# The scan's first token: VectorE's addition in PSUM replaced by a state from GpSimd that ScalarE copies in

## The chip, the cores and the metric

The kernel runs on one core of a Trainium2 chip. A core has five engines with a queue each: TensorE (PE in the profile, PEld for its weight loads), VectorE (DVE), ScalarE (ACT), GpSimd (POOL) and SyncE (SP), whose queue issues the DMAs here. Each queue is worked off in order; the engines meet only at semaphores. Matmul results land in PSUM; everything else lives in SBUF. The metric is the device time of one execution in microseconds, the median of several runs. A time of this kernel is told from no change at about 0.2%.

## The reference: what is computed

A state-space layer, then a gated feed-forward layer, each with a residual and a layer norm. For two sequences of 1024 tokens, model width 512 and state width N = 128:

```
xn    = rmsnorm(x) * norm_w ;  xn = xn * sigmoid((xn @ sel.T + b) * gate)
delta, B, C = split(xn @ x_proj.T)              # 128, 128, 128 wide
dt    = softplus(delta @ dt_proj.T + dt_b)      # 512 wide
A     = -exp(A_log)                             # 512 x 128
h_t   = exp(dt_t * A) * h_(t-1) + (dt_t * xn_t) B_t^T     # 512 x 128 per token
y_t   = h_t C_t
x     = layernorm(x + (y + x * D_param) @ out_proj.T)
x     = layernorm(x + (silu(x @ wg.T) * (x @ wu.T)) @ wd.T)   # hidden 2048
```

The state `h` is zero at the start of each sequence. All is fp32.

## The kernel before

**Tiling of the scan.** State column n lies on the partition, so a scan instruction has 128 partitions. Time is cut into 64 steps of S = 32 tokens (32 steps per sequence). A step `st` has two halves `i`, a half covers 256 of the 512 channels, and a half is worked in 8 iterations `r` = 0..7 of 32 channels each. The main loop thus has 1024 iterations `k`; here "half-step" means 8 of them. In one scan instruction (L660) 32 channels x 32 tokens lie one behind the other, 1024 elements. So that a channel does not run on into the next, the decay factor of each first token in `a_sb` is zero; the scan therefore starts every channel from the first token's entry in `bu`, and what the previous step left must already be in that entry.

**One iteration.** TensorE makes two things, each in two matmuls of 512 columns that sit in 32-row groups: `bu` (L644) from the diagonal tiles `du` and the row tile `ub`, and the exponent's argument `a` (L377) for the *next* iteration from `ddt` and `a_t`. Their order in the queue is bu, a, bu, a; this is called a block below. ScalarE turns `a` into decay factors in two `Exp` instructions (L384) into one of three buffers of `a_sb`, tokens 1 to 31 only. VectorE adds the carried state into the first token of `bu` in PSUM (L657, 128x32), then scans (L660) into `h`. Four PSUM banks hold two buffers of `bu` (L644 of iteration k+2 must wait for the scan of k), and two banks hold `a` (a matmul must wait for the Exp of the same half of the iteration before).

**The carried state.** `load(st)` (L302 on) fetches for the next step the rows `ub` (eight DMAs, L310 and L313) and `cd`, the first token's `dt` spread over 128 partitions (L320), and copies C into `cz` (L315). `carry_a` makes `cd = exp(a_n * cd)`: a product on GpSimd (L326) and an Exp on ScalarE (L327), at iteration 5 of the first half. `carry_h` (L335) multiplies half of `cd` by the last token of `h` of the step before, on GpSimd, at iteration 1 of the half ahead of the one that needs it. L657 adds a slice of the product. The first step of each sequence (`st % NSB == 0`) carries nothing and has no L657.

**Other work.** GpSimd builds `ddt` and `du` (L348, L358): one 128x512 product per iteration, two of each kind in four iterations. `y_round` (L396) multiplies finished states by `cz` at iterations 1, 4 and 7 of the next half. A hand-written list of generators, `work`, fills TensorE's remaining time: `PARTS = (4, 0, 3, 3, 0, 3, 3, 0)` says how many parts (matmuls, roughly) are taken after each iteration's block, with a credit that carries over up to 6. A generator yields `"H"` between parts, `"E"` where other engines must act first, `"P"` where it wants the one spare PSUM bank. Through it run `pre` (the projections of the next 256 tokens, 8 chunks; the B projection is L240 with the copy L246), `post` (L429 to L459) and `ffn` (L469 on: `gu` L500, `d` L518, `silu`). The order on every queue is the order in which this program issues; nothing reorders it.

Of the kernel before, what the change touches and what calls it, by code (L numbers as in the profile page):

```python
# [9 lines left out]
FP = mybir.dt.float32  # L10
AF = mybir.ActivationFunctionType
ALU = mybir.AluOpType
# [3 lines left out]
P = 128  # L16
S = 32
TC = 256
# [16 lines left out]
def kernel(  # L35
# [17 lines left out]
    nc = tc.nc  # L53
# [3 lines left out]
    B, L, D = out.shape  # L57
    NTT = B * L // P
    N = a_log.shape[2]
    R = dtw_t.shape[0]  # L60
    NF = wgu_s.shape[0]
    NM = D // P
    NH = NF // 2
    NJ = TC // P
    HD = D // 2
    NSB = L // S
    NS = B * NSB
    SPC = TC // S
# [10 lines left out]
    u_d = dram.tile([B * L, D], FP, name="u_d")  # L79
# [29 lines left out]
    xp_w = main.tile([P, NM, R + 2 * N], FP, name="xp_w")  # L109
# [6 lines left out]
    pre_pool = tc.alloc_tile_pool(name="pre", bufs=1)  # L116
    step_pool = tc.alloc_tile_pool(name="step", bufs=2)
# [34 lines left out]
    made = {}  # L152
# [3 lines left out]
    def misc(name):  # L156
        return bank_pool[0].tile([P, 512], FP, tag="m", name=name)
# [5 lines left out]
    def pre(c):  # L163
# [7 lines left out]
        low = pre_pool.tile([P, TC], FP, tag="low", name=f"low_{c}")  # L171
        dt = pre_pool.tile([P, NM, TC], FP, tag="dt", name=f"dt_{c}", bufs=2)
        u = pre_pool.tile([P, NM, TC], FP, tag="u", name=f"u_{c}")
        c_sb = pre_pool.tile([P, TC], FP, tag="c_sb", name=f"c_sb_{c}", bufs=2)
        made[c] = dt, c_sb
        xn = xT

        def matmuls(ps, w, m, rhs):
# [13 lines left out]
        ps = misc(f"ss_{c}")  # L192
# [19 lines left out]
        for m in range(NM):  # L212
            ps = misc(f"sel_{c}_{m}")
# [17 lines left out]
        for g, dst in ((0, low), (2, c_sb)):  # L231
            ps = misc(f"xp_{c}_{g}")
# [4 lines left out]
        ps = misc(f"b_{c}")  # L237
        for j in range(NJ):
            for k in range(NM):
                nc.tensor.matmul(  # L240
                    ps[:, ts(j, N)], xn[:, k, ts(j, P)], xp_w[:, k, R : R + N],
                    start=(k == 0), stop=(k == NM - 1),
                )
            yield "H" if j + 1 < NJ else "E"
        bt = pre_pool.tile([P, NJ, N], FP, tag="bt", name=f"bt_{c}")
        nc.scalar.copy(bt, ps[:, 0:TC].rearrange("p (j n) -> p j n", j=NJ))  # L246
        nc.sync.dma_start(b_d[ts(c, TC), :].rearrange("(j p) n -> p j n", p=P), bt)
        yield "P"

        for a in range(0, NM, 2):  # L250
            ps = misc(f"z_{c}_{a}")
# [14 lines left out]
        for j in range(NJ):  # L266
            yield "P"
            ps = misc(f"uT_{c}_{j}")
# [5 lines left out]
            t = pre_pool.tile([P, D], FP, tag="row", name=f"uT_{c}_{j}")  # L274
# [3 lines left out]
        ps = misc(f"t0_{c}")  # L278
        for m in range(NM):
# [3 lines left out]
                start=True, stop=True,  # L283
            )
        yield "E"
        t = pre_pool.tile([P, D], FP, tag="row", name=f"t0_{c}")
# [12 lines left out]
    def toks(st):  # L299
        return ts(st % SPC, S)  # L300

    prepared, carried, dus, ddts, hs, ys = {}, {}, {}, {}, {}, {}  # L302

    def load(st):


        ub = step_pool.tile([P, 2, P], FP, tag="ub", name=f"ub_{st}")
        rows = u_d[ts(st, S), :].rearrange("t (m g c) -> g t m c", g=4, c=32)
        for g in range(4):
            nc.sync.dma_start(  # L310
                ub[ts(g, S), 0, :].rearrange("t (m c) -> t m c", c=32), rows[g]
            )
            nc.sync.dma_start(ub[ts(g, S), 1, :], b_d[ts(st, S), :])  # L313
        prepared[st] = ub
        nc.gpsimd.tensor_copy(  # L315
            cz[st % 3][:, 28:284].rearrange("p (b w) -> p b w", w=32)[:, :, 0:4],
            made[st // SPC][1][:, toks(st)].rearrange("p (b t) -> p b t", t=4),
        )
        cd = step_pool.tile([P, D], FP, tag="cd", name=f"cd_{st}")
        nc.sync.dma_start(cd, dt0_d[st : st + 1, :].to_broadcast([P, D]))  # L320
        carried[st] = cd

    def carry_a(st):

        cd = carried[st]
        nc.gpsimd.tensor_tensor(cd, a_n, cd, ALU.mult)  # L326
        nc.scalar.activation(cd, cd, AF.Exp)  # L327

    def carry_h(st, i):

        if st % NSB == 0:
            return
        cd = carried[st].rearrange("p (b i e) -> p b i e", i=2, e=16)[:, :, i, :]
        last = hs[2 * (st - 1) + i][:, :, S - 1].rearrange("p (b e) -> p b e", e=16)
        nc.gpsimd.tensor_tensor(cd, cd, last, ALU.mult)  # L335

    def diag(j, part):

        h, a = j // 2, 2 * (j % 2)
        if h >= 2 * NS:  # L340
            return
        st, i = divmod(h, 2)
        name, m = divmod(part, 2)
        shape = [P, 2, 16, S]
        if name == 0:
            if m == 0:
                ddts[j] = half_pool.tile(shape, FP, tag="ddt", name=f"ddt_{j}")
            nc.gpsimd.tensor_tensor(  # L348
                ddts[j][:, m, :, :],
                made[st // SPC][0][:, a + m, toks(st)].unsqueeze(1).to_broadcast([P, 16, S]),  # L350
                hot[:, ts(i, 16)].unsqueeze(2).to_broadcast([P, 16, S]),
                ALU.mult,
            )
        else:
            if m == 0:
                dus[j] = half_pool.tile(shape, FP, tag="du", name=f"du_{j}")
            uv = prepared[st][:, 0, :].rearrange("p (m i e) -> p m i e", i=2, e=16)[:, :, i, :]
            nc.gpsimd.tensor_tensor(  # L358
                dus[j][:, m, :, :],
                uv[:, a + m, :].unsqueeze(2).to_broadcast([P, 16, S]),  # L360
                hot.unsqueeze(1).to_broadcast([P, 16, S]),
                ALU.mult,
            )
# [3 lines left out]
    def place(k):  # L367
        h, r = divmod(k, 8)
        m, pair = divmod(r, 2)
        return h, m, pair  # L370

    def decay_mm(k, b):

        h, m, pair = place(k)
        g = 2 * pair + b
        ps = ps_a.tile([P, 16, S], FP, tag="a", name=f"a_{k}_{b}")
        nc.tensor.matmul(  # L377
            ps, a_t[ts(g, 32), m, :], ddts[k // 4][ts(g, 32), m % 2, :, :],
            start=True, stop=True,
        )  # L380
        return ps

    def decay_exp(k, b, ps):
        nc.scalar.activation(  # L384
            a_sb[:, k % 3, ts(b, 16), 1:], ps[:, :, 1:], AF.Exp
        )
# [235 lines left out]
    for k in range(NG):  # L622
        h, m, pair = place(k)
        st, i = divmod(h, 2)
        r = k % 8
        work.others()
        if r == 0:
            hs[h] = half_pool.tile([P, 256, S], FP, tag="h", name=f"h_{h}")

            if i == 1 and st:  # L630
                y_out(st - 1)
            if i == 0:
                if st % SPC == 0 and st // SPC + 1 < NC:
                    pres[st // SPC + 1] = work.add(pre(st // SPC + 1), front=True)
                if st + 1 < NS:
                    if (st + 1) % SPC == 0:
                        work.finish(pres[(st + 1) // SPC])
                    load(st + 1)

        bu = ps_bu.tile([P, 32, S], FP, tag="bu", name=f"bu_{k}")  # L640
        nxt = []
        for b in range(2):
            g = 2 * pair + b
            nc.tensor.matmul(  # L644
                bu[:, ts(b, 16), :], prepared[st][ts(g, 32), 1, :],
                dus[k // 4][ts(g, 32), m % 2, :, :],
                start=True, stop=True,
            )
            if k + 1 < NG:
                nxt.append(decay_mm(k + 1, b))  # L650
        if nxt:
            decay_exp(k + 1, 0, nxt[0])
        if st % NSB:
            left = carried[st].rearrange("p (b i e) -> p b i e", i=2, e=16)
            first = bu[:, :, 0].rearrange("p (b e) -> p b e", e=16)
            at = 4 * m + 2 * pair
            nc.vector.tensor_tensor(first, first, left[:, at : at + 2, i, :], ALU.add)  # L657
        if nxt:
            decay_exp(k + 1, 1, nxt[1])
        nc.vector.tensor_tensor_scan(  # L660
            hs[h][:, ts(r, 32), :].rearrange("p q t -> p (q t)"),
            a_sb[:, k % 3, :, :].rearrange("p q t -> p (q t)"),
            bu.rearrange("p q t -> p (q t)"),
            0.0, ALU.mult, ALU.add,
        )
        if h:
            for b in ROUNDS[r]:
                y_round(h - 1, b)
        credit = min(credit + PARTS[r], 6)
        while PARTS[r] and credit > 0 and work.tensor():  # L670
            credit -= 1

        j, r4 = divmod(k, 4)
        if r4 == 3:
            diag(j + 2, 0)
        else:
            diag(j + 1, r4 + 1)
        if r == 1:
            if i == 0 and st:
                carry_h(st, 1)  # L680
            if i == 1 and st + 1 < NS:
                carry_h(st + 1, 0)
        if r == 5 and i == 0 and st + 1 < NS:
            carry_a(st + 1)
# [81 lines left out]
```

## Time and profile before

Median of three runs 2960.17 us (2959.35 to 2963.21).

| | |
|---|---|
| profiled execution, its own time | 2962.62 us |
| its span | 2960.8 us |
| TensorE busy | 2757.0 us (93%) |
| VectorE busy | 2526.3 us (85%), of it the scan 2340.8 (1024 x 2287 ns) and the addition L657 183.7 (992 x 185 ns) |
| GpSimd busy | 1842.1 us (62%) |
| ScalarE busy | 1545.2 us (52%), of it the Exps of `a_sb` 1089.4 |
| first scan starts, last scan ends | 97.7, 2847 us |

How to read it: the span has a head of 98 us (the first chunk's projections, no scan), a loop of 2750 us, and a tail of 113 us in which TensorE finishes the feed-forward layer alone. In the loop, up to about 475 us, there is no feed-forward work yet; after that TensorE has side work in nearly every half-step. Busy shares are averages over these stages.

### The profile page before, as it was taken

What the parts mean: (1) busy time and instruction counts of PE and PEld (TensorE: products, weight loads), DVE (VectorE), ACT (ScalarE), POOL (GpSimd) and SP (SyncE); (2) the same over time, 40 slices, a digit from 0 to 9 for tenths busy, and PEclk for the clock granted to TensorE, in tenths of its full rate; (3) what the DMA queues carried; (4) which work ended last, traced back from release to release, by engine and by line L of the source; (5) the groups of instructions that cost most, each with busy time, mean ns of one, the idle gap of its engine ahead of it and who ended that gap; (6) DMA issues with size and microseconds to landing.
All of it is one profiled execution on the core that took longest, in us unless ns stands there. A gap on an engine that the chain in (4) does not pass through costs nothing.

```text
span 2960.8 us, 53130 instructions
## 1 busy us (share of the span) xinstructions
PE 2757.0 (93%) x20608; PEld 1388.5 (47%) x20608; DVE 2526.3 (85%) x2176; ACT 1545.2 (52%) x3043; POOL 1842.1 (62%) x1970
## 2 busy tenths in 40 slices
PE   3787779999999998999999999999999999999988
PEld 2332324545444444444444454444444545454457
DVE  0599999999888998999999999999998999999940
ACT  2454445645465464664555555555555545454533
POOL 2465556766657575675666766576666757665744
PEclk7699999999999999999999999999999999999999
DMA  1000001212112111112111111111211212122123
GB/s 60 26 19 19 11 26 37 62 62 61 35 49 65 46 61 41 50 55 69 46 47 60 54 58 60 49 51 38 76 47 39 74 54 62 49 61 63 55 79 121
DMA packets 110458, 155.11 MB, mean 52 GB/s; under 512 B 46784, under 2 KB 69824, under 8 KB 110208
## 3 DMA queue, kind: packets, MB, share of 16 engines
q1 hardware_dynamic: 110208, 151.72, 16.7%
q8 instruction: 164, 2.69, 0.4%
q14 instruction: 86, 0.70, 0.1%
HBM read 142.09 MB, written 9.57 MB: 51 GB/s over the span
## 4 chain that ended last, share of the span: by engine, by line
PE 70%; DVE 20%; issue 4%; POOL 2%; ACT 2%; DMA 1%; SPq 0%; DVEq 0%; POOLq 0%; ACTq 0%
PE bu L644 25%; DVE h L660 17%; PE gu L500 16%; PE y L396 12%; PE d L518 6%; PE a L377 5%; PE sel L180 1%; DVE bu L657 1%; PE op L443 1%; PE xp L180 1%; ACT a_sb L384 1%; PE b L240 1%; PE ss L194 0%; DMA w<-in_wd_s_dram 0%; POOL dt L296 0%
## 5 line engine op out<-in xcount | busy, mean ns | idle before, releaser
L660 DVE TENSOR_TENSOR_SCAN h<-a_sb,bu 128x1024 f32<-128x1024 f32 x1024 | 2340.8, 2287 | 217.0 <-PE bu L644 100.0
L384 ACT ACTIVATE a_sb<-a 128x496 f32<-128x496 f32 x2048 | 1089.4, 585 | 1129.7 <-PE a L377 976.1
L644 PE MATMUL bu<-du,ub 32*128 32x512 f32 x4096 | 1213.5, 648 | 77.2 <-DVE h L660 43.7
L377 PE MATMUL a<-ddt,a_t 32*128 32x512 f32 x4096 | 1262.6, 649 | 13.4 <-POOL ddt L348 12.8
L348 POOL TENSOR_TENSOR ddt<-dt,hot 128x512 f32<-128x512 f32 x512 | 534.6, 1050 | 337.4 <-PE a L377 337.3
L358 POOL TENSOR_TENSOR du<-ub,hot 128x512 f32<-128x512 f32 x512 | 535.9, 1052 | 52.0 <-PE a L377 49.5
L644 PEld LDWEIGHTS bu<-du,ub 32*128 32x128 f32 x4096 | 343.9, 185 | 477.7 <-issue 283.7
L396 PE MATMUL y<-h,cz 128*32 128x256 f32 x8192 | 531.1, 389 | 1.6 <-DVE h L660 1.6
L500 PE MATMUL gu<-x1T,w 128*128 128x256 f32 x2048 | 518.7, 395 | 5.7 <-ACT x1T L488 2.8
L500 PEld LDWEIGHTS gu<-x1T,w 128*128 128x128 f32 x2048 | 368.7, 190 | 253.2 <-issue 178.3
L396 PEld LDWEIGHTS y<-h,cz 128*32 128x32 f32 x8192 | 229.6, 110 | 415.8 <-issue 305.6
L377 PEld LDWEIGHTS a<-ddt,a_t 32*128 32x128 f32 x4096 | 384.5, 185 | 42.1 <-ACT a_sb L384 21.8
L534 POOL TENSOR_SCALAR gu<-gu 128x256 f32<-128x256 f32 x128 | 108.7, 849 | 314.0 <-ACT gu L506 313.9
L518 PE MATMUL d<-w,hid 128*128 128x256 f32 x1024 | 261.8, 397 | 20.2 <-DMA w<-in_wd_s_dram 10.0
L657 DVE TENSOR_TENSOR bu<-bu,cd 128x32 f32<-128x32 f32 x992 | 183.7, 185 | 111.9 <-PE a L377 106.9
L518 PEld LDWEIGHTS d<-w,hid 128*128 128x128 f32 x1024 | 185.6, 192 | 145.5 <-issue 92.3
L410 POOL TENSOR_TENSOR yc<-yc,pick 128x512 f32<-128x512 f32 x64 | 66.6, 1041 | 155.9 <-ACT yc L409 155.9
L335 POOL TENSOR_TENSOR cd<-cd,h 128x256 f32<-128x256 f32 x124 | 106.6, 859 | 64.3 <-DVE h L660 64.3
L540 POOL TENSOR_TENSOR hid<-gu,e 128x256 f32<-128x256 f32 x128 | 93.6, 731 | 26.5 <-ACT e L539 23.9
L524 DVE TENSOR_TENSOR x<-x,d 128x256 f32<-128x256 f32 x64 | 25.5, 399 | 94.3 <-PE d L518 94.3
L535 POOL TENSOR_TENSOR gu<-gu 128x256 f32<-128x256 f32 x128 | 94.5, 738 | 10.7
L506 ACT COPY gu<-gu 128x512 f32<-128x512 f32 x128 | 75.3, 588 | 38.9 <-PE gu L500 38.9
(86 smaller groups left out, 1292.0 us busy)
## 6 DMA issues: line engine op xcount, KB each, us to landing
w<-in_wgu_s_dram SPq DMA_DIRECT2D x128, 512.0 KB, 4.1
w<-in_wd_s_dram SPq DMA_DIRECT2D x64, 512.0 KB, 4.1
cd<-dt_d SPq DMA_DIRECT2D x64, 256.0 KB, 4.3
xT<-in_x_t_dram SPq DMA_DIRECT2D x8, 512.0 KB, 5.2
u_d<-uT SPq DMA_DIRECT2D x16, 256.0 KB, 2.2
ub<-u_d SPq DMA_DIRECT2D x256, 16.0 KB, 2.0
ub<-b_d SPq DMA_DIRECT2D x256, 16.0 KB, 1.9
zT<-in_x_q_dram SPq DMA_DIRECT2D x16, 256.0 KB, 5.9
```

What stands on the lines that cost most here:

```text
L335: nc.gpsimd.tensor_tensor(cd, cd, last, ALU.mult)
L348: nc.gpsimd.tensor_tensor(ddts[j][:, m, :, :], made[st // SPC][0][:, a + m, toks(st)].unsqueeze(1).to_broadcast([P, 16, S]), hot[:, ts(i, ...
L358: nc.gpsimd.tensor_tensor(dus[j][:, m, :, :], uv[:, a + m, :].unsqueeze(2).to_broadcast([P, 16, S]), hot.unsqueeze(1).to_broadcast([P, 16, ...
L377: nc.tensor.matmul(ps, a_t[ts(g, 32), m, :], ddts[k // 4][ts(g, 32), m % 2, :, :], start=True, stop=True,)
L384: nc.scalar.activation(a_sb[:, k % 3, ts(b, 16), 1:], ps[:, :, 1:], AF.Exp)
L396: nc.tensor.matmul(ys[st][ts(m, 32), ts(i, 256)], cz[st % 3][:, at : at + 32], hs[h][:, ts(m, 64), ts(b, 4)], start=(i == 0 and b == 0), s ...
L500: nc.tensor.matmul(ps[:, ts(a, TC)], w[:, a, k, :], x1T[:, k, :], start=(k == 0), stop=(k == NM - 1),)
L518: nc.tensor.matmul(ps[:, 0:HD], hid[:, f, ts(j, P)], w[:, f % 4, :], start=(f == 0), stop=(f == NH - 1),)
L534: nc.gpsimd.tensor_scalar_max(g, g, -80.0)
L644: nc.tensor.matmul(bu[:, ts(b, 16), :], prepared[st][ts(g, 32), 1, :], dus[k // 4][ts(g, 32), m % 2, :, :], start=True, stop=True,)
L657: nc.vector.tensor_tensor(first, first, left[:, at : at + 2, i, :], ALU.add)
L660: nc.vector.tensor_tensor_scan(hs[h][:, ts(r, 32), :].rearrange("p q t -> p (q t)"), a_sb[:, k % 3, :, :].rearrange("p q t -> p (q t)"), b ...
```

## The change

The first token's complete state is now made ahead. TensorE multiplies, in a third group at the end of the B projection, each step's first token alone: four matmuls with 8 moving columns per chunk, into 8 spare columns of the same bank; the group before it now yields `"H"` and takes one more part. ScalarE copies the 8 columns to `b0` (128x8). `load` fetches `cu`, the first token's row of `u = dt * xn`, spread over 128 partitions (one more 256 KB DMA per step on SP's queue). `carry_a` scales `cu` by the step's column of `b0` on ScalarE, ahead of the Exp of `cd`. `carry_h` adds the product to `cu` on GpSimd. In the loop ScalarE copies the slice of `cu` over the first token of `bu`, between its two Exps, in all 1024 iterations; the matmuls of `bu` keep all 512 columns and TensorE's other groups are kept. `made[c]` becomes a triple, so `load` reads C from index 2.

```
+        b0 = pre_pool.tile([P, SPC], FP, tag="b0", name=f"b0_{c}", bufs=2)
-        made[c] = dt, c_sb
+        made[c] = dt, b0, c_sb
...
-            yield "H" if j + 1 < NJ else "E"
+            yield "H"
+        for k in range(NM):
+            nc.tensor.matmul(
+                ps[:, TC : TC + SPC], xp_w[:, k, R : R + N],
+                xn[:, k, :].rearrange("p (s t) -> p s t", t=S)[:, :, 0],
+                start=(k == 0), stop=(k == NM - 1),
+            )
+        yield "E"
...
+        nc.scalar.copy(b0, ps[:, TC : TC + SPC])
...
+        cu = step_pool.tile([P, D], FP, tag="cu", name=f"cu_{st}")
         nc.sync.dma_start(cd, dt0_d[st : st + 1, :].to_broadcast([P, D]))
-        carried[st] = cd
+        nc.sync.dma_start(cu, u_d[st * S : st * S + 1, :].to_broadcast([P, D]))
+        carried[st] = cd, cu
...
         nc.gpsimd.tensor_tensor(cd, a_n, cd, ALU.mult)
+        nc.scalar.activation(cu, cu, AF.Copy, scale=b0[:, st % SPC : st % SPC + 1])
         nc.scalar.activation(cd, cd, AF.Exp)
...
         nc.gpsimd.tensor_tensor(cd, cd, last, ALU.mult)
+        nc.gpsimd.tensor_tensor(cu, cu, cd, ALU.add)
...
-        if st % NSB:
-            left = carried[st].rearrange("p (b i e) -> p b i e", i=2, e=16)
-            first = bu[:, :, 0].rearrange("p (b e) -> p b e", e=16)
-            at = 4 * m + 2 * pair
-            nc.vector.tensor_tensor(first, first, left[:, at : at + 2, i, :], ALU.add)
+        h0 = carried[st][1].rearrange("p (b i e) -> p b i e", i=2, e=16)
+        first = 4 * m + 2 * pair
+        nc.scalar.copy(
+            bu[:, :, 0].rearrange("p (b e) -> p b e", e=16), h0[:, first : first + 2, i, :]
+        )
```

More of the change, by code (lines that the diff above doesn't have):

```diff
@@ L316, in load @@
             cz[st % 3][:, 28:284].rearrange("p (b w) -> p b w", w=32)[:, :, 0:4],
-            made[st // SPC][1][:, toks(st)].rearrange("p (b t) -> p b t", t=4),
+            made[st // SPC][2][:, toks(st)].rearrange("p (b t) -> p b t", t=4),
         )
         cd = step_pool.tile([P, D], FP, tag="cd", name=f"cd_{st}")
+        cu = step_pool.tile([P, D], FP, tag="cu", name=f"cu_{st}")
         nc.sync.dma_start(cd, dt0_d[st : st + 1, :].to_broadcast([P, D]))
-        carried[st] = cd
+        nc.sync.dma_start(cu, u_d[st * S : st * S + 1, :].to_broadcast([P, D]))
+        carried[st] = cd, cu
     def carry_a(st):
-        cd = carried[st]
+        cd, cu = carried[st]
+        b0 = made[st // SPC][1]
         nc.gpsimd.tensor_tensor(cd, a_n, cd, ALU.mult)
+        nc.scalar.activation(cu, cu, AF.Copy, scale=b0[:, st % SPC : st % SPC + 1])
         nc.scalar.activation(cd, cd, AF.Exp)
@@ L332, in carry_h @@
             return
-        cd = carried[st].rearrange("p (b i e) -> p b i e", i=2, e=16)[:, :, i, :]
+        cd, cu = (t.rearrange("p (b i e) -> p b i e", i=2, e=16)[:, :, i, :] for t in carried[st])
         last = hs[2 * (st - 1) + i][:, :, S - 1].rearrange("p (b e) -> p b e", e=16)
         nc.gpsimd.tensor_tensor(cd, cd, last, ALU.mult)
+        nc.gpsimd.tensor_tensor(cu, cu, cd, ALU.add)
     def diag(j, part):
```

## The prediction

> **What bounds the kernel now.** I read the page first, then the list of waits, then the busy times by stage, then the timelines of single engines around one half-step. From the page:
>
> ```profile
> span 2960.8 us, 53130 instructions
> PE 2757.0 (93%) x20608; PEld 1388.5 (47%) x20608; DVE 2526.3 (85%) x2176; ACT 1545.2 (52%) x3043; POOL 1842.1 (62%) x1970
> PE 70%; DVE 20%; issue 4%; POOL 2%; ACT 2%; DMA 1%; SPq 0%; DVEq 0%; POOLq 0%; ACTq 0%
> ```
>
> VectorE is busy 85% of the span but carries 20% of the chain that ended last; TensorE carries 70%. The stages explain it (columns: stretch, length, then busy time of PE, PEld, DVE, ACT, POOL):
>
> ```profile
> 97.70:474.60 376.90, 319.31 (x2413) 131.98 (x2414) 346.27 (x282) 186.77 (x357) 210.03 (x215) 0.92 0.06 16
> 474.60:2848.00 2373.40, 2305.12 (x17618) 1150.61 (x17614) 2171.31 (x1876) 1300.19 (x2570) 1552.18 (x1655) 1.00 0.18 54
> ```
>
> Up to 475 us VectorE is busy 92% and TensorE 85%; later TensorE is idle only 68 of 2373 us. So an addition less on VectorE can pay in full in the first stage only, and in the second no more than TensorE's waits for VectorE.
>
> What the addition costs is seen where a sequence ends, at 1473 us; the first step of the second sequence has none:
>
> ```profile
> 1471.16 2.29 DVE L660 TENSOR_TENSOR_SCAN h<-a_sb,bu 128x1024 f32<-128x1024 f32 x1
> 1473.43 0.20 DVE L657 TENSOR_TENSOR bu<-bu,cd 128x32 f32<-128x32 f32 x1
> 1473.73 4.46 DVE L660 TENSOR_TENSOR_SCAN h<-a_sb,bu 128x1024 f32<-128x1024 f32 x2
> ```
>
> Two scans back to back take 4.46 us, so the second starts 2.17 us after the first; with the addition between, scans of a busy VectorE start 2.48 us apart (10 of 128 half-steps hold no side work; nine of them last 19.85 to 20.48 us). An addition is worth 0.31 us where VectorE leads.
>
> What ScalarE's side looks like, in a half-step with feed-forward work. First ScalarE's timeline, then the chain (start, us, what):
>
> ```profile
> 1053.74 1.06 ACT L384 ACTIVATE a_sb<-a 128x496 f32<-128x496 f32 x2 [1.43 <-PE a L377]
> 1054.68 0.63 ACT L327 ACTIVATE cd<-cd 128x512 f32<-128x512 f32 x1
> 1055.20 0.59 ACT L506 COPY gu<-gu 128x512 f32<-128x512 f32 x1
> 1055.67 1.08 ACT L384 ACTIVATE a_sb<-a 128x496 f32<-128x496 f32 x2
> ```
> ```profile
> 1053.68 0.63 PE gu L500 x2
> 1054.31 0.62 PE bu L644
> 1054.93 0.14 PE a L377
> ...
> 1055.50 0.47 PE a L377
> 1055.97 2.36 PE gu L500 x10
> ```
>
> This block lasts 1.66 us, from 1054.31 to 1055.97; others last 1.07. Its second `a` waits for the bank that the second Exp, ending at 1054.80, frees; 1.17 us after that the block is over. So TensorE already waits here for the second Exp, and the change puts a copy ahead of just that Exp. Counted over the timeline, 271 of the 879 blocks after the first 18 half-steps end 1.17 to 1.18 us after that Exp, and a further 285 between 1.35 and 1.50: the first kind has no slack, the second 0.18 to 0.33. The list of waits names few of them (wait, total us, times, longest), for a row-group matmul runs meanwhile and TensorE counts as busy:
>
> ```profile
> PEld a L377 <- ACT a_sb L384: 21.8, 80, 1.0
> DVE bu L657 <- PE a L377: 106.9, 166, 8.2
> ```
>
> **The change, part by part.**
>
> *1. The addition goes, first stage.* By the lists of instructions all 992 leave VectorE and nothing enters there. Half-steps 2 to 17 (145 to 475 us) hold 128 of them, 115 started with VectorE not idle. With scans 2.17 us apart the next limit is the round trip: a scan ends, 0.05 us later the block that reuses its bank starts, 1.14 us, 0.04 us, the first Exp 0.585, the copy 0.2, 0.06: 2.07 us, plus the scan's 2.29, gives 4.36 us for two iterations, 2.18 for one. After the two long `y` rounds (1.43 us each) the block comes about 0.4 us late, so a half-step would last 8 x 2.18 + 0.7 = 18.1 against 19.85. But 31 of these 128 blocks take over 1.6 us (the granted clock is 0.92 in this stage), and those show once VectorE is no slower. 16 x 1.75 = 28 less about 6: -22. Bounds: -35 (115 x 0.31) and -8 (the slow blocks eat most).
>
> *2. The addition goes, later.* VectorE's scan leads 13.7% of the chain there, but a gain ends where TensorE never idles. TensorE's rows show for it 8.5 + 7.0 us ahead of `bu`, 6.5 + 1.0 ahead of `d`, 4.6 ahead of `zT`, 3.9 of `op`, some 3 more: 35 us. The `d` and `zT` waits hang on additions that stay. I take -15; bounds -35 and 0.
>
> *3. The copy, 1024 times, between the Exps.* No row of before shows 128x32 on ScalarE. Nearest rows: a 128x1 ACTIVATE takes 203 ns (L560), a 128x496 Exp 585, a 128x256 copy 372. ScalarE's instructions overlap: two Exps take 1.06, so the second starts 0.475 after the first, 0.11 before its end, and so do the mixed neighbours above (1054.68, 1055.20). So the copy takes 0.2 and holds up the next by 0.10 (bounds 0.08 with this overlap, 0.2 without). 271 blocks x 0.10 = 27, of which some 14% lie where VectorE leads: +24. At 0.08 it is 18, at 0.2, where the second kind of block begins to wait, 56.
>
> *4. `cu` scaled on ScalarE,* 64 times, just ahead of the `cd` Exp, a 128x512 row of 0.63, 0.52 with overlap. In the timeline above ScalarE has no gap from 1053.74 to 1058.1: the next Exps would start 0.6 us later. What waits for them is the next block but one, two `gu` groups later, so mostly hidden; where the side work behind iterations 5 or 6 is short (two of five patterns), it shows. Half-covered, in a third of the steps: 64 x 0.2 = +12; bounds 0 and 37.
>
> *5. The scan starts later when TensorE leads.* Now it starts 0.41 us after its block; then after the first Exp and the copy: 0.04 + 0.475 + 0.2 + 0.06 = 0.78. The bank is wanted again two blocks on; at 1054.31 the earlier scan had ended 0.44 us before, elsewhere in this half-step 1.0 to 1.9. It fits. What does not are 55 additions of `d` results (L524), queued behind that scan while the only spare bank waits for them: half of 55 x 0.37 = +9; bounds 0 and 22.
>
> *6. `b0`.* Eight chunks, 4 more matmuls, 8 rows each; the 8-row group L280 next to it has 91 ns weight loads, L240 186. Some 0.13 us a row, 1 us a chunk where TensorE leads; in the head, slow clock and a ScalarE copy more in the line: 2. +8; bounds 4 and 14.
>
> *7. The rest.* GpSimd: 124 additions like L335 (859 ns), 107 us; its products `du` are ready 4.9 us or more before their block nine times in ten, and `carry_h` ends 12.7 us or more before its half-step: nothing, 5 if that cover went. SP: one issue of 0.36 us and a 256 KB landing of 4.3 per step, ahead of weight fetches; `d` waited for weights in two places (10.0 us): +3, bounds 0 and 6. The one part more shifts the side work's pattern: 12 half-steps instead of 5 get an even one that lasted 0.4 us less: -3.
>
> Sum: -22 - 15 + 24 + 12 + 9 + 8 + 3 - 3 = +16 on the profiled execution's 2962.6, so 2978.6. That execution was 2.4 above the median of the runs: 2976.
>
> *A rule against the rows.* The Trainium skill, "ScalarE: Activation LUTs", section "What ACT_TABLE_LOAD costs", gives 186 ns + 0.833 ns per element and an overlap of 93 ns: 213 for the copy, 120 of delay, where the rows say 100. By it term 3 would be 28. The same page's "Rules for kernel authors" sends additions and products to VectorE and not ScalarE, which speaks against the change; here VectorE's addition (185 ns) and ScalarE's copy would cost about the same, and it is the place in the queue that differs.
>
> **Rivals.**
> - *VectorE's relief wins.* For it: VectorE's queue is never idle in 817 of 992 cases before the addition. Terms 1 and 2 near their ends (-30, -30) and 3 to 7 low (18 + 0 + 2 + 5 + 1 - 3): -37, 2923; at half of that, 2942. It decides when term 3 stays under 20 and `cu` is hidden. Against it: the steady half-steps' chain is TensorE alone.
> - *ScalarE becomes the late one.* A copy stands behind all that ScalarE has queued (three `silu` activations, 1.4 us; relu and abs of `pre`), and the scan now waits at once, where an Exp had an iteration in hand. If one iteration in six loses 0.37 us on the path, 170 x 0.37 = 63 more: 3040.
> - *Nothing.* The terms cancel: 2960. The removed time sits where TensorE hides it, the added in ScalarE's idle 48%.
> - That the addition remains is excluded by the instruction lists.
>
> **How the numbers follow.** My case (+7 to +50) 0.42; ScalarE late (over +50) 0.14; nothing (within 0.2%, 6 us, which a measurement can hardly tell from no change) 0.14; VectorE's relief (under -6) 0.30. So slower 0.56, same 0.14, faster 0.30. The range 2932 to 3022 leaves out the ends of the two outer cases; my case's own is 2967 to 3010.
>
> **What would show it.** Scans 2.2 us apart and half-steps near 18.3 us before 475 us; steady half-steps 0.2 to 0.4 us longer than the 21.1 of before; a copy row near 200 ns; "PE or PEld a <- ACT a_sb" growing from 22 us; VectorE waiting for ScalarE's copy instead of for `a`. I am wrong if steady half-steps keep their length, or if the first stage does not shrink.

## The result, and the profile after

The changed kernel takes **2996.0 us** (median of four runs, 2987.5 to 2998.4) against 2959.8 us for the kernel before, run beside it. The ratio is 1.0118, with a 95% interval of 1.0094 to 1.0141: slower by some 36 us. The forecast was 2976, slower by 16. Direction and range held; the loss is more than twice what was forecast.

From the page of the changed kernel:

```profile
span 2996.6 us, 53059 instructions
PE 2808.5 (94%) x20672; PEld 1422.4 (47%) x20672; DVE 2370.2 (79%) x1184; ACT 1697.1 (57%) x4139; POOL 1928.4 (64%) x2094
PE 74%; DVE 13%; ACT 5%; issue 4%; POOL 3%; DMA 1%; SPq 0%; POOLq 0%; ACTq 0%; DVEq 0%
L674 DVE TENSOR_TENSOR_SCAN h<-a_sb,bu 128x1024 f32<-128x1024 f32 x1024 | 2313.3, 2280 | 520.3 <-ACT bu L669 515.0
L669 ACT COPY bu<-cu 128x32 f32<-128x32 f32 x1024 | 200.5, 196 | 1.4 <-PE bu L658 1.4
```

VectorE is busy 156 us less, and its share of the chain fell from 20% to 13%. ScalarE's share of the chain rose from 2% to 5%. The copy takes 196 ns, as the 200 of the forecast. VectorE's scan now waits 520 us in all, 515 of them for the copy (96 of these in the head); before, VectorE waited 107 us ahead of its additions for TensorE and 100 us ahead of scans, 98 of these in the head.

The stages (columns as in the prediction: stretch, length, busy time of PE, PEld, DVE, ACT, POOL, then TensorE's granted clock):

```profile
96.40:462.70 366.30, 324.36 (x2415) 139.00 (x2414) 325.15 (x153) 206.80 (x507) 220.90 (x231) 0.93 0.08 22
462.70:2882.00 2419.30, 2348.97 (x17656) 1175.54 (x17654) 2035.48 (x1012) 1430.74 (x3511) 1627.14 (x1763) 0.99 0.19 59
```

The first stage is 10.6 us shorter, the later one 46 us longer. In the later stage TensorE is busy 44 us more and idle about as long as before (70 for 68 us).

Where VectorE leads, scans do stand 2.2 us apart, for a while. VectorE's timeline in half-step 11 (start, length, what, and in brackets the idle time ahead and what ended it):

```profile
329.21 6.64 DVE L674 TENSOR_TENSOR_SCAN h<-a_sb,bu 128x1024 f32<-128x1024 f32 x3 [0.38 <-ACT bu L669]
336.05 4.46 DVE L674 TENSOR_TENSOR_SCAN h<-a_sb,bu 128x1024 f32<-128x1024 f32 x2 [0.20 <-ACT bu L669]
```

Three scans in 6.64 us, then a gap that ScalarE's copy ends. Half-steps 5, 6, 11 and 14 last 18.25 to 18.38 us, close to the 18.1 that was worked out; the other twelve of half-steps 2 to 17 last 18.9 to 22.6.

Where TensorE leads, ScalarE's timeline and the chain show a block of the kind that the prediction showed of before, with two `gu` matmuls ahead of it:

```profile
1054.29 0.58 ACT L398 ACTIVATE a_sb<-a 128x496 f32<-128x496 f32 x1 [1.38 <-PE a L391]
1054.77 0.19 ACT L669 COPY bu<-cu 128x32 f32<-128x32 f32 x1
1054.88 0.59 ACT L398 ACTIVATE a_sb<-a 128x496 f32<-128x496 f32 x1
```
```profile
1054.23 0.63 PE gu L514 x2
...
1054.86 0.66 PE bu L658
1055.53 0.09 PE a L391
...
1056.05 0.58 PE a L391 x2
1056.63 1.43 PE y L410 x24
```

The second Exp starts 0.59 us after the first, where it was 0.475 (in the median of all iterations 0.587 and 0.481), and the block, from 1054.86 to 1056.63, lasts 1.77 us where its like lasted 1.66. The delay is 0.11 us, where 0.10 was forecast. Over all blocks after half-step 17 whose matmuls run at full speed, the time above 1.14 us grows from 85.8 to 111.9 us: 26 us, against 24 forecast. So the forecast's largest loss is there at its size, and something else is missing.

From the list of waits of the changed kernel (wait, total us, times, longest):

```profile
DVE h L674 <- ACT bu L669: 515.0, 603, 96.4
PEld a L391 <- ACT a_sb L398: 34.2, 124, 1.0
```

### The profile page after: what moved, and what is told of

The parts are those of the page before. It is cut to its first block, busy times and chain, and to the rows that moved or that the text cites. A ratio compares the mean times of both kernels' runs of the same rounds, so it can differ in the third digit from the quotient of the medians.

```text
span 2996.6 us, 53059 instructions
## 1 busy us (share of the span) xinstructions
PE 2808.5 (94%) x20672; PEld 1422.4 (47%) x20672; DVE 2370.2 (79%) x1184; ACT 1697.1 (57%) x4139; POOL 1928.4 (64%) x2094
## 4 chain that ended last, share of the span: by engine, by line
PE 74%; DVE 13%; ACT 5%; issue 4%; POOL 3%; DMA 1%; SPq 0%; POOLq 0%; ACTq 0%; DVEq 0%
PE bu L658 26%; PE gu L514 15%; PE y L410 14%; DVE h L674 12%; PE d L532 7%; PE a L391 6%; PE op L457 2%; PE sel L181 2%; PE xp L181 1%; ACT a_sb L398 1%; ACT bu L669 1%; PE ss L195 1%; PE b L241 1%; POOL du L372 0%; POOL dt L305 0%
## 5 line engine op out<-in xcount | busy, mean ns | idle before, releaser
L674 DVE TENSOR_TENSOR_SCAN h<-a_sb,bu 128x1024 f32<-128x1024 f32 x1024 | 2313.3, 2280 | 520.3 <-ACT bu L669 515.0
L398 ACT ACTIVATE a_sb<-a 128x496 f32<-128x496 f32 x2048 | 1206.3, 591 | 1021.1 <-PE a L391 848.4
L391 PE MATMUL a<-ddt,a_t 32*128 32x512 f32 x4096 | 1307.1, 649 | 14.4 <-POOL ddt L362 13.4
L514 PE MATMUL gu<-x1T,w 128*128 128x256 f32 x2048 | 525.4, 399 | 20.2 <-DMA w<-in_wgu_s_dram 4.9
L391 PEld LDWEIGHTS a<-ddt,a_t 32*128 32x128 f32 x4096 | 410.6, 185 | 56.0 <-ACT a_sb L398 34.2
L669 ACT COPY bu<-cu 128x32 f32<-128x32 f32 x1024 | 200.5, 196 | 1.4 <-PE bu L658 1.4
```

Of the source, the lines that this page charges most:

```text
L391: nc.tensor.matmul(ps, a_t[ts(g, 32), m, :], ddts[k // 4][ts(g, 32), m % 2, :, :], start=True, stop=True,)
L398: nc.scalar.activation(a_sb[:, k % 3, ts(b, 16), 1:], ps[:, :, 1:], AF.Exp)
L514: nc.tensor.matmul(ps[:, ts(a, TC)], w[:, a, k, :], x1T[:, k, :], start=(k == 0), stop=(k == NM - 1),)
L669: nc.scalar.copy(bu[:, :, 0].rearrange("p (b e) -> p b e", e=16), h0[:, first : first + 2, i, :])
L674: nc.vector.tensor_tensor_scan(hs[h][:, ts(r, 32), :].rearrange("p q t -> p (q t)"), a_sb[:, k % 3, :, :].rearrange("p q t -> p (q t)"), b ...
```

## The experiments

Theory "queue": the copy's place ahead of the second Exp is what costs. Its rivals: "scan waits" (the scan starts late because it waits for ScalarE), "preparation" (making `cu` costs), and "shift" (the side work's new part moves pauses of TensorE). Most of the runs below change one thing, and their code is shown shortened. Where half-steps are compared, their lengths are taken between starts of scans in the profiled execution and summed; "first stage" is half-steps 2 to 17, "later" is 18 to 126. Each comparison was timed beside the kernel before, which stayed between 2959 and 2962 us.

### The addition alone

```diff
-        if st % NSB:
-            left = ...
-            nc.vector.tensor_tensor(first, first, left[...], ALU.add)
```

> The kernel before with VectorE's 992 additions of the carried state left out and nothing put in their place (the output lacks what one step carries to the next); everything that prepares the state stays. This is the gain that the change could have had at most. Theory 'queue' (the copy ahead of the second Exp eats the gain): half-steps 2 to 17 shrink by 25 to 30 us, the later ones by 5 to 15, together 2920 to 2930. Theory 'no gain to be had' (slow blocks fill the gap at once): the first stage shrinks by 11 as in the changed kernel, the rest by nothing, 2948.

Measured: **2903.5 us**, ratio 0.9811 (0.9797 to 0.9825). First stage -35.5 us, later -19.0. The gain that lay in the addition is 56 us, more than either theory gave. The busy times of the first stage and TensorE's waits for VectorE in it (us, times, longest), before and then without the addition:

```profile
144.60:474.60 330.00, 273.09 (x2180) 109.14 (x2184) 309.96 (x265) 160.93 (x308) 187.94 (x193) 0.94 0.07 18
PE bu L644 <- DVE h L660: 34.9, 36, 1.6
PE bu L644 <- DVE bu L657: 20.9, 25, 1.3
```
```profile
136.80:431.40 294.60, 269.54 (x2174) 117.21 (x2175) 286.17 (x138) 160.53 (x305) 187.25 (x193) 1.00 0.07 20
PE bu L644 <- DVE h L655: 24.4, 59, 1.0
```

TensorE's granted clock is 0.94 before and 1.00 without the addition. Summed over stretches of 10 us as length times (1 - granted clock), TensorE loses 20.4 us to the lower clock in the first stage before, and 0.0 here; its waits for VectorE fall from 55.8 to 24.4 us.

The slow blocks that were expected to eat part of the gain were of two kinds. Of the 31 that last over 1.6 us before, 12 have matmuls at half clock, and 19 wait for the second Exp of the block before. Without the addition there are again 31, all of the second kind, and what they cost does not show: VectorE is busy 286 of 294.6 us. That the gain of 35.5 us equals 115 x 0.31 us is in part chance. Half-steps 10 to 15 hold one stretch of half clock each (a slow spell) and go from 20.48 to some 17.5 us, more than eight additions are worth; half-steps 2 and 17 gain only 0.3 us each.

### A copy that nothing waits for

```diff
+        nc.scalar.copy(spare, hot)        # 128x32, between the two Exps
```

> The kernel before, its additions kept, with one ScalarE copy of 128x32 in each of the 1024 iterations between the two Exps, from a constant to a spare tile, which nothing waits for. Theory 'queue': each of the some 270 blocks whose end is set by the second Exp gets 0.10 us longer, +28 us, nothing in the first stage where VectorE leads: 2985 to 2995. Theory 'preparation' (b0, the DMA of cu, its scaling cost the time): +0 to +5, below 2966. Theory 'scan start' (the scan's wait for the copy costs): +0 to +10.

Measured: **2983.7 us**, ratio 1.0081 (1.0069 to 1.0094); +1.2 in the first stage, +20.2 later. ScalarE's time between the Exps costs 24 us by itself, spread over all of the later half-steps. That is just under what "queue" gave, and far above "preparation" and "scan start".

### `b0` alone

```diff
+            yield "H"
+        for k in range(NM):  nc.tensor.matmul(ps[:, TC : TC + SPC], ...)
+        nc.scalar.copy(b0, ps[:, TC : TC + SPC])
```

> The kernel before with only the matmuls and the copy of b0 added, in a part of their own (the result is not used). Work alone: 32 rows of 4 matmuls, 7.7 us, of which 7 on TensorE's path: 2967. Theory 'shift' (the one part more moves side work against the blocks and so makes pauses of TensorE, after which it runs at half its clock): +15 to +25, with more slow spells than the five of before.

Measured: **2954.3 us**, ratio 0.9987 (0.9978 to 0.9996). Not slower, rather some 4 us faster, which is near the limit of what can be told from no change. Half-steps 64 to 79 do get a new pause for weights (4.4 us in the list of waits; these half-steps are 11.9 us longer in all), but the other later ones are 16 us shorter. So a shift of the side work moves pauses about, and here its balance is no loss.

### All of the preparation, the copy on VectorE

```diff
-        nc.scalar.copy(
+        nc.vector.tensor_copy(
             bu[:, :, 0].rearrange(...), h0[...]
```

> The changed kernel with the copy to PSUM made by VectorE, where the addition was, instead of ScalarE: all of the preparation (b0, the DMA of cu, its scaling, GpSimd's additions) and none of the rest. Theory 'queue': VectorE works as long as before, so the preparation alone shows, b0 7 and scaling up to 12: 2965 to 2980. Theory 'preparation': 2995 or more, as with the copy on ScalarE. Theory 'shift': 2975 to 2990 with as many slow spells as e3.

Measured: **2979.9 us**, ratio 1.0070 (1.0056 to 1.0084). VectorE's copy takes 184 ns, as its addition did (185), so the preparation costs 20 us; the forecast's terms for it (12 + 8 + 3 - 3) also make 20.

### The changed kernel without its copies

```diff
-        nc.scalar.copy(
-            bu[:, :, 0].rearrange(...), h0[...]
-        )
```

> The changed kernel without its 1024 copies to PSUM (the output lacks what one step carries to the next), all preparation kept. Without the addition alone the time was 2903, and the preparation alone cost 20. Theory 'sum': the two add up, 2924, half-steps 2 to 17 some 33 us shorter than before; so the copies cost the changed kernel 72. Theory 'overlap' (the preparation costs more where VectorE no longer covers it): 2935 to 2950, and the copies cost 45 to 60.

Measured: **2926.0 us**, ratio 0.9890 (0.9873 to 0.9907). The sum of the two earlier results was 2924, so gain and preparation add up. The 1024 copies therefore cost the changed kernel 70 us, though all of them together take 200.5 us on an engine that is idle 43% of the span.

### The same, with a copy that nothing waits for

```diff
-        nc.scalar.copy(bu[:, :, 0].rearrange(...), h0[...])
+        nc.scalar.copy(spare, hot)
```

> The changed kernel with each copy kept at its place between the two Exps and of its size, but from a constant to a spare tile in SBUF, so that the scan does not wait for it and it waits for nothing (the output lacks the carried state). Against the kernel without any copy it shows ScalarE's time alone, against the changed kernel what the scan's wait for the copy costs. Theory 'queue' (the delay of the second Exp is the cost): within 10 us of the changed kernel, 2986 to 2996. Theory 'scan waits': +24 over the kernel without copies, as with the idle copy in the kernel before, about 2948, half-steps 2 to 17 still some 30 us shorter than before; the remaining 48 us come from the scan that starts after ScalarE.

Measured: **2957.3 us**, ratio 0.9996 (0.9987 to 1.0005). So 31 us of the 70 are ScalarE's time, and **39 us are the wait of the scan for the copy**: this kernel and the changed one issue the same instructions, and differ only in what the copy reads and writes and who waits for it. The copy takes 210 ns here and 196 in the changed kernel, and the second Exp starts 0.59 us after the first in both:

```profile
L670 ACT COPY spare<-hot 128x32 f32<-128x32 f32 x1024 | 215.2, 210 | 0.0
```

The first stage, in this kernel and then in the changed one:

```profile
143.50:447.00 303.50, 290.17 (x2181) 122.77 (x2182) 287.69 (x136) 179.34 (x443) 198.84 (x209) 1.00 0.09 26
```
```profile
144.10:462.70 318.60, 278.93 (x2184) 116.91 (x2184) 288.82 (x138) 178.99 (x441) 198.88 (x209) 0.96 0.09 25
```

Fifteen of the 39 us are here. TensorE is idle 13 us in the one and 40 in the other, and the clock is 1.00 against 0.96. How the two belong together is seen in TensorE's timeline of the changed kernel:

```profile
347.11 0.69 PE L658 MATMUL bu<-du,ub 32*128 32x512 f32 x1 [0.46 <-DVE h L674]
...
349.84 1.19 PE L658 MATMUL bu<-du,ub 32*128 32x512 f32 x1 [0.79 <-DVE h L674]
...
350.83 1.05 PE L658 MATMUL bu<-du,ub 32*128 32x512 f32 x1
...
351.86 2.11 PE L410 MATMUL y<-h,cz 128*32 128x256 f32 x24
353.90 0.69 PE L658 MATMUL bu<-du,ub 32*128 32x512 f32 x1
```

TensorE pauses 0.46 and 0.79 us for scans that ended late, and then runs at half speed (granted clock 0.51 from 349.7 to 353.1): a matmul of 0.69 us takes 1.19, the `y` round of 1.43 takes 2.1. The block ends a microsecond later, the scan after it waits 0.81 us, and the next pause, of 0.70 us, follows at 358.15.

The other 27 us are in the later stage (the two profiled executions stand 42 us apart, the medians 39). Median time from the end of a block's last `bu` matmul to the start of its scan there: 0.18 us in the kernel whose scan waits for no copy, 0.78 in the changed one. In the kernel before it was 0.74, between 0.41 and more than 1 us, as the scan often stood behind the scan before and an addition. What waits for VectorE there, first without and then with that wait:

```profile
PE d L533 <- DVE x L539: 2.8, 7, 0.4
PE zT L444 <- DVE x L539: 2.6, 7, 0.4
PE op L458 <- DVE zT L449: 2.1, 3, 0.7
PE bu L659 <- DVE h L673: 0.8, 3, 0.4
```
```profile
PE d L532 <- DVE x L538: 6.9, 7, 1.0
PE zT L443 <- DVE x L538: 6.8, 7, 1.0
PE bu L658 <- DVE h L674: 4.6, 10, 0.8
PE op L457 <- DVE zT L448: 3.8, 3, 1.3
```

Everything that VectorE does for the side work stands behind a scan that starts 0.6 us later. These four rows grow by 14 us, TensorE's idle time in all by 23 (47 to 70 us), and the time lost to the lower clock from 10.3 to 23.8 us (the two overlap, since a slow spell follows a pause).

The Trainium skill, "TensorE: Matmul & The Clock Gate", section "What's actually happening", puts the fall to half clock after an idle window of about 3.4 us. The half speed agrees with the trace; the condition does not, since no pause in the stretch above is longer than 0.79 us. Here the measurement decides. But such pauses do not always bring a slow spell. The same pair stands earlier in the same profile, at a granted clock of 1.00, and the `y` round behind it takes 1.50 us:

```profile
229.74 0.69 PE L658 MATMUL bu<-du,ub 32*128 32x512 f32 x1 [0.46 <-DVE h L674]
...
232.47 0.66 PE L658 MATMUL bu<-du,ub 32*128 32x512 f32 x1 [0.79 <-DVE h L674]
...
233.54 1.50 PE L410 MATMUL y<-h,cz 128*32 128x256 f32 x24
```

The eight slow spells of this stage last 3.41 us each, and they begin whole multiples of 3.41 us apart (151.8, 182.5, 250.7 us and so on). So it may matter how pauses fall into such stretches; no run tests it.

### The copy behind both Exps

```diff
-            decay_exp(k + 1, 0, ...); copy; decay_exp(k + 1, 1, ...)
+            decay_exp(k + 1, 0, ...); decay_exp(k + 1, 1, ...); copy
```

> The changed kernel with the copy behind both Exps instead of between them. The second Exp is not delayed, the scan starts some 0.5 us later. Theory 'queue': the 0.10 us per block are gone, 24 to 28 us less, about 2970. Theory 'scan waits': the round trip of a bank grows from 4.36 to 4.84 us for two iterations, half-steps 2 to 17 by 0.24 x 8 = 1.9 us each, +30 there, and later half-steps become bound by it too: 3020 or more.

Measured: **3036.3 us**, ratio 1.0260 (1.0244 to 1.0276); the first stage is 12.4 us longer than before, the later one 61.5. "Queue" said 2970 and is refuted as the main cause. Scans now start 1.26 us after their block, and that costs 40 us more although the second Exp is no longer held up. With the same preparation and the same instructions, starts at 0.18, 0.78 and 1.26 us go with 2957, 2996 and 3036 us. TensorE's wait for the bank in the first stage is 64.3 us (38.5 in the changed kernel), and 28.9 us are lost there to the lower clock:

```profile
PE bu L658 <- DVE h L674: 64.3, 59, 1.6
```

### `b0` without a part of its own

```diff
-            yield "H"
+            if j + 1 < NJ:
+                yield "H"
```

> The changed kernel with the four matmuls of b0 in the same part of the side work as the last group of b, so that the side work has as many parts as before. Theory 'shift': half-steps 64 to 79 lose the pause for weights that both kernels with the additional part show there (+12 and +19 to +20 us), and fewer slow spells of TensorE remain than nine: 2975 to 2982. Theory 'no shift': the time stays within 5 us of the changed kernel, since other pauses come in its place.

Measured: **2995.6 us**, ratio 1.0131 (1.0111 to 1.0151): no difference. In its profiled execution, 11 us above its median, half-steps 64 to 79 are 12 us shorter than in the changed kernel and the other later ones 22 us longer. "Shift" is not the cause. The pauses for weights fall elsewhere, and there is about as much of them either way: in the later half-steps TensorE waits 10.1 us for weights here, 9.6 in the changed kernel and 10.0 before.

### The copy one iteration ahead

```diff
+            decay_exp(k + 1, 1, nxt[1])
+            first_token(k + 1)      # allocates bu of k + 1 and copies to [:, :, 0]
-                bu[:, ts(b, 16), :], ..., dus[...][..., :, :]
+                bu[:, ts(b, 16), 1:], ..., dus[...][..., :, 1:]
```

> The changed kernel with the same copy made one iteration ahead: it stands behind the second Exp of the iteration before and writes the first token's column as soon as the scan of two iterations back has left the bank; the product matmuls then write only the 31 other columns of each segment, so neither the scan nor an Exp waits behind the copy. Theory 'scan waits' with 'queue' (31 us from ScalarE's place between the Exps, 39 us from the scan's wait): both go, and the time is that of the kernel without copies, 2926, with half-steps 2 to 17 some 31 us shorter than before; scans start 0.18 us after their block as there. Theory 'the wait only moves' (ScalarE now stands waiting for a scan, and what is queued behind it comes late): 2955 to 2975.

Measured: **3042.4 us**, ratio 1.0281 (1.0259 to 1.0302), the slowest of all, beyond what either theory gave. Scans do start 0.18 us after their block, but the block itself now waits. The longest entry of TensorE's waits, and ScalarE's timeline ahead of a block that starts at 317.94:

```profile
PE bu L672 <- ACT bu L644: 202.8, 332, 2.2
```
```profile
316.73 1.06 ACT L398 ACTIVATE a_sb<-a 128x496 f32<-128x496 f32 x2 [2.71 <-PE a L391]
317.68 0.21 ACT L644 COPY bu<-cu 128x32 f32<-128x32 f32 x1
```

The matmuls that write the other 31 columns wait for the copy all the same, and the copy stands behind two Exps that wait for the block before. So the wait moved from VectorE to TensorE, 202.8 us in all, and the kernel is 46 us slower than the changed one.

### The smaller matmul alone

```diff
-                bu[:, ts(b, 16), :], ..., dus[...][..., :, :]
+                bu[:, ts(b, 16), 1:], ..., dus[...][..., :, 1:]
```

> The changed kernel with its copy where it is, but product matmuls of 31 columns per segment as in the kernel with the copy ahead: what the smaller matmul alone gives, so that the two can be told apart. Theory 'scan waits': the copy still stands behind the first Exp and the scan behind the copy, so 2990 to 2998. If the matmul's size counts in full (16 of 512 columns of a 0.59 us matmul, twice in 1024 iterations): 2958.

Measured: **2980.7 us**, ratio 1.0078 (1.0065 to 1.0091): 15 us less than the changed kernel, more than "scan waits" gave (6 at most) and less than the matmul's size in full (38). Seven of them are in the first stage. From the start of a block to the start of its scan it takes 1.89 us in the median, for 1.92 in the changed kernel: a small step on the same trip.

### `cu` scaled by GpSimd

```diff
-        nc.scalar.activation(cu, cu, AF.Copy, scale=b0[...])
+        nc.gpsimd.tensor_scalar(cu, cu, b0[...], None, ALU.mult)
```

> The changed kernel with cu scaled by GpSimd instead of ScalarE (64 instructions). The preparation cost 20 us in all; b0 alone did not make the kernel before slower. Theory 'scaling': ScalarE's 64 x 0.72 us are exposed in part and go: 2978 to 2985. Theory 'DMA and GpSimd' (the preparation's cost lies in the transfer and in GpSimd's additions): 2993 to 3000.

Measured: **2972.3 us**, ratio 1.0052 (1.0036 to 1.0068): 24 us less, twice the forecast's term of 12. ScalarE's timeline in the changed kernel:

```profile
1060.26 0.72 ACT L339 ACTIVATE cu<-cu,b 128x512 f32<-128x512 f32 x1
1061.70 0.63 ACT L340 ACTIVATE cd<-cd 128x512 f32<-128x512 f32 x1 [0.72 <-POOL cd L338]
```

The scaling takes 0.72 us, not the 0.63 of its neighbour, and the next Exps and copy stand behind both instructions. On GpSimd the same scaling takes 1.57 us, and the lists of waits name nothing that waits for it.

### Both together

> The changed kernel with both edits that took time off it: product matmuls of 31 columns per segment (-15 alone) and cu scaled by GpSimd (-24 alone). If they lie on different paths they add up: 2996 - 39 = 2957, no difference to the kernel before. If both only give back the same slack (the same pauses of TensorE and the same slow spells), less than 30 together: 2966 or more.

Measured: **2969.7 us**, ratio 1.0029 (1.0017 to 1.0041): 26 us less than the changed kernel, not 39. So the two edits give back partly the same time; which time they share was not looked into.

### The copy's way in the first stage only

```diff
+    def early(st):
+        return 0 < st < SPC
...
+            if early(st):
+                nc.scalar.copy(first, left[:, at : at + 2, i, :])
+            else:
+                nc.vector.tensor_tensor(first, first, left[:, at : at + 2, i, :], ALU.add)
```

> The changed kernel's way (b0, cu, GpSimd's addition, ScalarE's copy) in steps 1 to 7 only, where VectorE leads (half-steps 2 to 15); VectorE's addition in all later steps, without cu and b0 there. From the changed kernel's own half-steps: 11 us less up to half-step 16, nothing later: 2945 to 2951. Rival 'the clock' (the later stage starts with a fuller clock or pauses move): outside that by more than 8 us.

Measured: **2945.4 us**, ratio 0.9952 (0.9938 to 0.9965), first stage -14.3, later -0.8. Faster than both kernels: the change pays where VectorE leads and is left out where TensorE leads.

With the 31 columns and the scaling on GpSimd in those steps:

> The copy's way in steps 1 to 7 only (2945 with the copy as in the changed kernel), there with 31 columns and the scaling on GpSimd, VectorE's addition in all later steps. If the first stage's loss against the kernel without copies is the round trip through ScalarE and the pauses with lowered clock that it leaves, a shorter trip gives 7 us for the columns and 6 for the scaling, the shares that these had in half-steps 2 to 17 of the whole kernel: 2932 to 2938, and less clock lost there than 11.9 us. If the trip doesn't matter: 2945.

Measured: **2937.3 us**, ratio 0.9919 (0.9901 to 0.9937), the fastest version here that computes all of the reference. First stage -22.3 us, and 5.1 us lost there to the lower clock, where the version above lost 11.9 and the changed kernel 13.6. TensorE waits for scans as long as in the version above, 37.7 and 37.8 us in this stage, so what pays is not fewer pauses; how much belongs to the clock and how much to the shorter trip through ScalarE was not separated.

## Why the prediction was wrong in its size

The chain of single steps, each measured, against the forecast's terms (each step starts from the kernel of the step above, so the measured sum closes by construction):

| step | forecast, us | measured, us | from |
|---|---|---|---|
| addition gone (terms 1 and 2) | -37 | -56 | without the addition, against before |
| preparation (terms 4, 6, 7) | +20 | +23 | changed without copies, against without the addition |
| copy's time between the Exps (term 3) | +24 | +31 | with the idle copy, against without copies |
| scan waits for the copy (term 5) | +9 | +39 | changed kernel, against the idle copy |
| sum | +16 | +37 | |

- **Term 5 failed: +9 was forecast, +39 measured.** It compared the scan's start of 0.78 us with the 0.41 that it had behind an addition, and let only the 55 additions of `d` pay for the 0.37. Measured against a scan that waits for nothing the copy costs 0.6 us, 0.78 for 0.18. And all of VectorE's work for the side groups stands behind the scan, `zT`, `op` and the transposes of `x` too, not `d` alone; the `d` rows account for 4 of the 39 us. The forecast's "it fits" holds for the bank: TensorE's wait for it in the later stage is only 4.6 us.
- **Terms 1, 2 and 5 belong together,** since term 5 was counted from the addition's place and the measured step from a scan that waits for nothing. Together they were -28 in the forecast and -17 measured: 11 of the 21 us that the forecast lacks. The copy's time gives another 7 and the preparation 3.
- **Term 1 was right in the trip and wrong in the slow blocks.** Clean half-steps came out at 18.25 to 18.38 for the 18.1 worked out. The forecast set all 31 beside the lower clock and let 6 us go for them; 19 of them wait for an Exp. Without the addition no block runs at half clock and the full 35 us appear; with the scan waiting for ScalarE eight do, and -22 became -11.4.
- **Term 2** was -15 against -19: right.
- **Term 3** was right in its mechanism and place. The delay is 0.11 us, between the 0.10 that it took and the 0.12 that was set beside it; 271 x 0.10 less 14% is 23, not 24. The copy added to the kernel before cost 24 us. In the changed kernel the copy costs 31, since VectorE no longer hides it in the first stage (+4.5 us there).
- **Terms 4, 6 and 7** were right in sum and wrong in their shares: scaling cost 24, not 12, and `b0` with its part brought -4 by itself, where +8 and -3 were forecast.
- Of the rivals, "ScalarE becomes the late one" named the mechanism that decided, the scan that waits at once for ScalarE, but put it at 63 us for ScalarE's backlog. It acts in most iterations instead (603 of 1024 scans wait for the copy in the list), by the plain order block, Exp, copy, scan.
- The shown signs held: scans 2.2 us apart and half-steps near 18.3 before 475 us (four of sixteen), a copy near 200 ns, later half-steps longer (median 21.15 to 21.50 us), the wait of `a` for ScalarE grown from 22 to 34 us, VectorE waiting for the copy.

Not separated: how the 39 us divide between TensorE's pauses and the lower clock that follows them.

## What to carry to other kernels

Price a moved operation in two steps, against the kernel with the operation gone: what leaving it out gives, and what every waiter pays for its new place. An engine that is idle 43% of the span still makes its result late if that result stands behind other work in its queue, and all that the waiting engine does for others becomes late with it. Make such a change only in the stage whose limit it relieves: here that turned +36 us into -14, and with a shorter trip into -24.

## What was not expected of the hardware

TensorE's clock fell to half for 3.4 us or twice that at a time: in the stretch shown behind pauses of 0.46 and 0.79 us, where the matmuls ahead used 32 rows; in the later stage of the changed kernel it did so behind single waits of 1.0 to 4.9 us. The same two short pauses elsewhere left it full, and the kernel without the addition kept it full in the first stage through 59 waits of up to 1.0 us. What decides was not found. In the first stage the lower clock lost 20.4 us before, 13.6 in the changed kernel, and 0.0 to 1.7 in the three kernels whose scan waited for neither an addition nor a copy.

Time at the lower clock is not time of the kernel one for one. Half-steps 10 to 15 of the kernel before hold one spell each, which loses 1.7 us of clock (3.41 x 0.5), and they last 20.48 us where half-steps without a spell or side work last 19.86: 0.6 us more.
